# Summing the state products of a selective scan: accumulating transfers in place of GpSimd additions

## The chip, the cores and the metric

The kernel runs on one core of a Trainium2 chip. The metric is the device time in microseconds, the median of several executions. The core has TensorE (PE in the profile), VectorE (DVE), ScalarE (ACT), GpSimd (POOL) and SyncE (SP, which here only issues transfers). Each engine runs its own instructions in the order in which they were recorded, and waits for others through semaphores. DMA engines move data beside them; a transfer is issued by an instruction on the queue of some engine and tells its landing by a semaphore.

## The reference

The input x is 4 sequences of 1024 tokens with 128 channels. Four blocks are added to it one after the other, each behind a layer norm: sparse attention, a feed-forward net with weights of plus and minus one, a Mamba block, and the same feed-forward net again. The change is in the scan of the Mamba block:

```
def step(h, inp):
    dt_t, B_t, C_t, u_t = inp
    dA = jnp.exp(dt_t[..., None] * A)
    h = dA * h + (dt_t * u_t)[..., None] * B_t[:, None, :]
    y_t = jnp.einsum('ben,bn->be', h, C_t)
    return (h, y_t)
...
y = ys.transpose(1, 0, 2) + u2 * D_param
y = y * jax.nn.silu(z)
out = jnp.einsum('ble,ed->bld', y, W_out)
return x + res_scale * out
```

There are E = 256 inner channels and N = 16 states. For each token and inner channel, y is the sum over the 16 states of state times C, plus the skip term u2 * D. All of it is float32.

## The kernel before

**Stages.** First comes the attention, up to about 245 us. After the weights of the other blocks are loaded, the first feed-forward pieces and the first Mamba inputs are made, and then the scan stage runs. All the rest of the work, most of the two feed-forward blocks and the Mamba projections among it, is put between the scans in small pieces. Behind the scans comes the last feed-forward batch, which needs the last scan's output.

**Units.** Inner channels lie on the 128 partitions in NH = 2 halves, and 512 tokens (CH) lie along the free axis. One unit is one state n of one half sequence (b, f): 4 sequences x 2 halves x 16 states = 128 units, in the order of `parts_in_order`, the state innermost. `scans` (from line 1134) records the units one after the other. In unit i:

- `load_b` (line 1142) issues on SP, every second unit, the transfer of two states' B rows to all partitions (`bs`, 512 KB).
- `drive(i + 2)` makes on GpSimd `db` = dt * u * B for two units ahead. There are three `db` buffers, so this product waits for the scans of unit i - 1.
- TensorE spreads the row of C over all partitions (`pcc`, one PSUM bank, so that it waits for the product of unit i - 1).
- VectorE runs two scans, one for each half: `hs` from `da` (PSUM, made by ScalarE in `decay`) and `db`.
- VectorE multiplies both halves at once: `hc` = `hs` * `pcc`, a tile of 128 x 1024 float32, 512 KB:

```
hss[i] = m2.tile([P, NH, CH], F32, name=f"hc{i}", tag="hc", bufs=6)
ve.tensor_tensor(hss[i], hs, pc.unsqueeze(1).to_broadcast([P, NH, CH]), ALU.mult)
```

**The sum over states.** Products are added in pairs. For an even unit k, `fold` adds `hc` of unit k into `hc` of unit k + 1 on GpSimd, one half at a time (128 x 512), in units k + 2 and k + 3. `total` then adds the pair's sum into a PSUM bank `pys` with a matmul by the identity, one half at a time, in units k + 3 and k + 4; the first addition of a half sequence is preceded by a matmul with `skip_d`, the skip term. After the 16th state `gated` multiplies `pys` into the gate tile on VectorE, in units k + 4 and k + 5 for the last pair. The gate then goes to the output projection (`mamba_out`, `mamba_out_own`).

**What sets the order.** The kernel's engines are wrapped so that instructions stay in the order recorded. Between a unit's scans and its product, and behind the product, `pieces` places side work. It keeps a modelled clock for each engine, which `spend` advances by the expected duration of what was recorded, and rates of side work that each engine is owed per unit (`RATES`, line 1278). So whatever changes the modelled clocks or the moment at which a gate is finished also changes where later pieces stand.

**Buffers.** The six `hc` buffers are handed out again in the order in which they are released, a buffer being released by the last recorded reader of its tile. PSUM has three banks for side work (`SPARE`), two for `da`, one for `pcc`, and one for each half's `pys`.

Of the kernel before, what the change touches and what calls it, by code (L numbers as in the profile page):

```python
# [16 lines left out]
F32 = mybir.dt.float32  # L17
# [5 lines left out]
ALU = mybir.AluOpType  # L23
# [3 lines left out]
P = 128  # L27
# [10 lines left out]
E, N, DC, DR = 256, 16, 4, 8  # L38
NH = E // P
CH = 512  # L40
# [3 lines left out]
def hybrid_kernel(ctx: ExitStack, tc: tile.TileContext, x, Wq, Wk, Wv, Wo, ln_g, ln_b, W_in, conv_w,  # L44
# [17 lines left out]
    ve, te, sc, gp = (InOrder(e) for e in (nc.vector, nc.tensor, nc.scalar, nc.gpsimd))  # L62
# [32 lines left out]
    ident = const.tile([P, P], F32, name="ident")  # L95
# [611 lines left out]
    with tc.tile_pool(name="kload", bufs=1) as kl:  # L707
# [7 lines left out]
        total = fw.tile([P, 1], F32, name="total")  # L715
# [16 lines left out]
    fed = set()  # L732
# [166 lines left out]
    skip_d = mw.tile([P, NH, P], F32, name="skip_d")  # L899
# [13 lines left out]
    units = [(b, f, n) for b, f in parts_in_order for n in range(N)]  # L913
    PER = N
    mamba_in, mamba_pre, prepared = {}, {}, set()
# [218 lines left out]
    def scans(wide, ready):  # L1134

        bss, dbs, das, hss = {}, {}, {}, {}
        py = {}
        last = len(units) - 1  # L1140

        def load_b(i):

            if i <= last and i % 2 == 0:
                b, f, n = units[i]
                ready(b, f, "b")
                bss[i] = m2.tile([P, 2, CH], F32, name=f"bs{i}", tag="bs", bufs=2)
                nc.sync.dma_start(bss[i], mamba_pre[b, f][5][n : n + 2, :].partition_broadcast(P))

        def drive(i):  # L1150
            if i <= last:
                b, f, n = units[i]
                ready(b, f, NH - 1)
                dbs[i] = m2.tile([P, NH, CH], F32, name=f"db{i}", tag="db", bufs=3)
                bs = bss[i - n % 2][:, n % 2]
                gp.tensor_tensor(dbs[i], mamba_pre[b, f][3], bs.unsqueeze(1).to_broadcast([P, NH, CH]), ALU.mult)

        def decay(i, h):
            if i <= last:
                b, f, n = units[i]  # L1160
                das[i, h] = wide.tile([P, CH], F32, name=f"da{i}_{h}", tag="da", bufs=2)
                sc.activation(das[i, h], mamba_pre[b, f][2][:, h], AF.Exp, scale=a_t[:, h, n : n + 1])

        def fold(i):

            h = i % 2
            k = i - 2 - h
            if 0 <= k <= last:
                gp.tensor_add(hss[k + 1][:, h], hss[k + 1][:, h], hss[k][:, h])

        def total(i):

            h = 1 - i % 2
            k = i - 3 - h
            if not 0 <= k <= last:
                return
            b, f, n = units[k]
            if n == 0:
                py[b, f, h] = wide.tile([P, CH], F32, name=f"pys{b}_{f}{h}", tag=f"pys{h}")
                te.matmul(py[b, f, h], skip_d[:, h], mamba_pre[b, f][1][:, h], start=True, stop=False)  # L1180
            te.matmul(py[b, f, h], ident, hss[k + 1][:, h], start=False, stop=n == N - 2)

        def gated(i):

            h = i % 2
            k = i - 4 - h
            if not 0 <= k <= last:
                return False
            b, f, n = units[k]
            if n == N - 2:  # L1190
                gate = mamba_pre[b, f][0]
                ve.tensor_mul(gate[:, h], gate[:, h], py.pop((b, f, h)))
                if h == NH - 1:
                    fed.add(("g", b, f))
            return n == N - 2


        done = {}

        def after(*keys):  # L1200
            return [done.get(k, 0.0) for k in keys]

        for i in range(3):
            load_b(i)
        for i in range(2):
            drive(i)
            done["db", i] = spend("gp", 2.38)
        for h in range(NH):
            decay(0, h)
            done["da", 0, h] = spend("sc", 0.7)  # L1210
        for i, (b, f, n) in enumerate(units):
            now[0] = i
            load_b(i + 3)
            fold(i)
            h0, h1 = i % 2, 1 - i % 2
            done["fold", i] = spend("gp", 1.29, *after(("hc", i - 1 - h0)))
            drive(i + 2)
            done["db", i + 2] = spend("gp", 2.38, *after(("hs", i - 1, 1)))
            pc = wide.tile([P, CH], F32, name=f"pcc{i}", tag="pcc")
            te.matmul(pc, spread[: 6 * N, n, :], mamba_pre[b, f][4], start=True, stop=True)  # L1220
            done["pcc", i] = spend("pe", 0.4, *after(("hc", i - 1)))
            hs = m2.tile([P, NH, CH], F32, name=f"hs{i}", tag="hs")
            db = dbs.pop(i)
            for h in range(NH):
                first = carry[b % 2][:, h, n : n + 1] if f else 0.0
                ve.tensor_tensor_scan(hs[:, h], das.pop((i, h)), db[:, h], first, ALU.mult, ALU.add)
                done["hs", i, h] = spend("ve", 1.235 if f else 1.175, *after(("da", i, h), ("db", i)))
            decay(i + 1, 0)
            done["da", i + 1, 0] = spend("sc", 0.67, *after(("hs", i, 0)))

            t = times["ve"]
            pieces(t + 2.5, lumps=False)
            if f == 0:
                sc.copy(carry[b % 2][:, :, n : n + 1], hs[:, :, CH - 1 :])
            decay(i + 1, 1)
            done["da", i + 1, 1] = spend("sc", 0.67 if f else 0.86, *after(("hs", i, 1)))
            if gated(i):
                spend("ve", 0.68, *after(("sum", i - 1)))
            hss[i] = m2.tile([P, NH, CH], F32, name=f"hc{i}", tag="hc", bufs=6)
            ve.tensor_tensor(hss[i], hs, pc.unsqueeze(1).to_broadcast([P, NH, CH]), ALU.mult)  # L1240
            done["hc", i] = spend("ve", 1.205, *after(("pcc", i)))
            total(i)
            done["sum", i] = spend("pe", 1.0, *after(("fold", i - 1)))
            t = times["ve"]
            pieces(t + 2.2)
        for i in range(last + 1, last + 6):
            fold(i)
            gated(i)
            total(i)


    SPARE = 3
# [3 lines left out]
    def spend(engine, us, *others):  # L1256
        times[engine] = max(times[engine], *others, 0.0) + us
        return times[engine]
# [36 lines left out]
    def pieces(until, lumps=True):  # L1295

        forced = not until
        evictions(lumps, forced)  # L1300
        for k, rate in RATES.items():
            owed[k] = min(max(owed[k], -2 * rate) + (0 if forced else rate / 2), rate / 2)
        left = SPARE - sum(w.held for w in works)

        for w in works[:-2] + sorted(works[-2:], key=lambda w: w.count):

            moved = w in emptied and now[0] < len(units) - 10
            while w.may() and not w.next.evict and w.next.banks <= left:
                if moved and not w.next.same and not (forced and w in emptied):
                    break  # L1310
                if not (forced or w.next.hurries()):
                    if any(us and owed[k] <= 0 for k, us in w.next.us.items()):
                        break
                    if "pe" in w.next.us and ends(w)[0]["pe"] > until:
                        break
                left -= w.next.banks
                issue(w)
                moved = True
            if forced and moved:
                break  # L1320

    def ready(*part):
        while part not in prepared:
            pieces(None)

    def stream(*kinds):
        for k in kinds:
            yield from k
# [23 lines left out]
    with banks(8):  # L1352
        first = [
            Work(stream(*(mamba_norm(0, c) for c in first_half))),
            Work(mamba_pre_half(*parts_in_order[0])),
        ]
# [18 lines left out]
    with banks(SPARE), tc.tile_pool(name="wide", bufs=1, space=PSUM) as wide:  # L1375
# [21 lines left out]
        ])  # L1397
        among_scans[0] = True
        scans(wide, ready)
        among_scans[0] = False  # L1400
        works.insert(0, Work(mamba_out_own(B - 1, 1)))
# [40 lines left out]
```

## Time and profile before

| | |
|---|---|
| runs | 905.14, 903.53, 904.64 us; median 904.64 |
| profiled execution, from the first to the last instruction | 901.9 us; of its own time outside the span nothing is recorded, and the median of the runs is 2.7 us above the span |
| busy: PE, DVE, ACT, POOL | 756.2, 754.3, 607.1, 727.0 us (84%, 84%, 67%, 81%) |
| `db` on POOL | 128 instructions, 2.363 us each |
| additions of pairs on POOL | 128 instructions, 1.272 us each |
| products `hc` on DVE | 128 instructions, 1.218 us each |
| scans on DVE | 256 instructions, 1.207 us (first half sequence) and 1.266 us (second) each |
| transfers of the 16 DMA engines | 53.18 MB; 20.4% of their time on the queue of SP, 0.2% on that of POOL |

In the rows, an instruction is named by engine, operation and tiles (out<-in). Nearly every one has line 57, since one helper records them all, so it is read by tiles. A float32 matmul of 512 columns is two records of PE. Instructions that issue a transfer are not counted as busy time of their engine. Times are from the span's start.

### The profile page before, as it was taken

Reading aid. Unit: us, or ns where it says so; the run is one execution under the profiler, and the core shown is the slowest. Engines: PE = TensorE matmul, PEld = TensorE weight load, DVE = VectorE, ACT = ScalarE, POOL = GpSimd, SP = SyncE. Lnnn points to the kernel's source line nnn. Section 1 sums busy time; section 2 is a strip of 40 time slices with the busy share of each in tenths; the row PEclk is TensorE's granted clock in tenths of the full one; section 3 lists DMA queues with packets and bytes.
Section 4 is the critical chain, followed back from the end, with each engine's and each line's share of the span. In section 5 each row is a group of like instructions: output and inputs, shape, how many; then the busy total and the mean of one; then the engine's idle time right before and its main releaser. Section 6 shows DMA issues by size and latency. Waiting matters only on the chain. (4 is left out here: it accounts for less than half of the span.)

```text
span 901.9 us, 16464 instructions
## 1 busy us (share of the span) xinstructions
PE 756.2 (84%) x6226; PEld 463.5 (51%) x6226; DVE 754.3 (84%) x994; ACT 607.1 (67%) x1358; POOL 727.0 (81%) x566
## 2 busy tenths in 40 slices
PE   5897779866798978879899888779889989989777
PEld 2454546544577642335456554335455545656457
DVE  6799999999533289798899999989988898999962
ACT  4776648744445488888787888888777766654423
POOL 6799958998322199999999999999988987997930
PEclk9899989987789997789999999899989999999899
DMA  4733123330100111121221211212111121221100
GB/s 127 131 73 70 43 44 69 72 65 2 43 7 1 49 53 66 67 74 48 70 69 51 70 48 70 72 47 72 70 72 59 53 78 59 70 82 58 60 7 19
DMA packets 47152, 53.18 MB, mean 59 GB/s; under 512 B 4808, under 2 KB 38384, under 8 KB 47072
## 3 DMA queue, kind: packets, MB, share of 16 engines
q1 hardware_dynamic: 45904, 51.59, 20.4%
q8 instruction: 49, 0.80, 0.4%
q0 software_dynamic: 608, 0.27, 0.2%
q10 hardware_dynamic: 560, 0.26, 0.1%
q14 instruction: 31, 0.25, 0.1%
HBM read 45.82 MB, written 4.46 MB: 56 GB/s over the span
## 5 line engine op out<-in xcount | busy, mean ns | idle before, releaser
L57 POOL TENSOR_TENSOR db<-du,bs 128x1024 f32<-128x1024 f32 x128 | 302.4, 2363 | 0.1
L57 ACT ACTIVATE da<-dt,a_t 128x512 f32<-128x512 f32 x256 | 175.5, 688 | 123.2 <-DVE hs L57 122.7
L57 POOL TENSOR_TENSOR hc<-hc,hc 128x512 f32<-128x512 f32 x128 | 162.8, 1272 | 29.1 <-DVE hc L57 28.8
L57 DVE TENSOR_TENSOR hc<-hs,pcc 128x1024 f32<-128x1024 f32 x128 | 155.9, 1218 | 23.7 <-PE pcc L57 15.4
L57 DVE TENSOR_TENSOR_SCAN hs<-da,db 128x512 f32<-128x512 f32 x128 | 149.4, 1207 | 20.7 <-ACT da L57 15.5
L57 DVE TENSOR_TENSOR_SCAN hs<-da,carry,db 128x512 f32<-128x512 f32 x128 | 156.9, 1266 | 1.2 <-ACT da L57 1.2
L57 PE MATMUL pys<-hc,ident 128*128 128x512 f32 x256 | 145.3, 651 | 6.1 <-POOL hc L57 6.0
L57 POOL TENSOR_TENSOR prodv<-vS,E 128x128 f32<-128x128 f32 (+14 forms) x30 | 69.3, 2311 | 11.5 <-ACT E L57 11.3
L57 PEld LDWEIGHTS pys<-hc,ident 128*128 128x128 f32 x256 | 49.8, 208 | 53.7 <-issue 28.1
L57 PE MATMUL pcc<-bc,spread 96*128 96x512 bf16 x128 | 51.5, 402 | 29.6 <-DVE hc L57 28.7
L57 PE MATMUL pga<-h1a,w 128*128 128x512 f32 x256 | 70.5, 425 | 2.7 <-DVE h1a L57 1.9
L57 POOL TENSOR_TENSOR prod<-kv,qs 128x128 f32<-128x128 f32 (+14 forms) x30 | 71.1, 2369 | 0.8 <-DVE or L57 0.8
L57 ACT ACT_TABLE_LOAD x48 | 61.6, 1283 | 3.5 <-issue 2.6
L57 PE MATMUL pc<-mxnT,w_conv 128*128 128x512 f32 x128 | 61.5, 606 | 2.0 <-ACT gate L57 2.0
L57 PEld LDWEIGHTS pga<-h1a,w 128*128 128x128 f32 x256 | 49.3, 195 | 25.5 <-issue 4.7
L57 ACT ACTIVATE E<-S 128x512 f32<-128x512 f32 (+15 forms) x62 | 26.5, 473 | 39.7 <-DVE S L57 39.5
L57 PE MATMUL ps<-kx,qT 64*32 64x256 f32 x1008 | 43.5, 416 | 5.8 <-DVE S L57 5.0
L57 POOL TENSOR_TENSOR du<-dt,u 128x512 f32<-128x512 f32 x16 | 20.4, 1275 | 30.5 <-ACT dt L57 30.5
L57 ACT COPY ep<-pt 128x512 f32<-128x512 f32 x32 | 18.7, 586 | 35.8 <-DVE eo L57 35.5
L57 PEld LDWEIGHTS pc<-mxnT,w_conv 128*128 128x128 f32 x128 | 24.6, 194 | 33.9 <-issue 26.7
L57 PE MATMUL pgb<-h1b,w 128*128 128x512 f32 x128 | 37.5, 439 | 4.8 <-DVE h1b L57 3.3
L57 PE MATMUL pgc<-h1c,w 128*128 128x256 f32 (+1 forms) x192 | 37.2, 346 | 0.0
(244 smaller groups left out, 1637.5 us busy)
## 6 DMA issues: line engine op xcount, KB each, us to landing
bs<-bd SPq DMA_DIRECT2D x64, 512.0 KB
vr<-vd SPq DMA_DIRECT2D x32, 256.0 KB
vd<-kv SPq DMA_DIRECT2D x8, 256.0 KB
x<-in_L_attn_a_x_dram SPq DMA_DIRECT2D x15, 128.0 KB
kx<-kT SPq DMA_DIRECT2D x104, 16.0 KB
out_dram<-x SPq DMA_DIRECT2D x8, 128.0 KB
taps<-in_L_attn_b_conv_w_dram SPq DMA_DIRECT2D x1, 512.0 KB
out_dram<-ox SPq DMA_DIRECT2D x2, 256.0 KB
```

The source lines that it names most:

```text
L57: ins = getattr(self.engine, name)(*args, **kwargs)
```

## The change

For units k to k + 3 with k divisible by four, three accumulating transfers issued on GpSimd's queue add the products, both halves at once (128 x 1024, 512 KB each): product k into k + 1 (issued in unit k + 2), k + 2 into k + 3 (unit k + 4), and then k + 1 into k + 3 (unit k + 6, which waits for the other two). They are recorded in `gather`, behind `drive`. `total` adds product k + 3, now the sum of four, into `pys`, half 0 in unit k + 7 and half 1 in unit k + 8. The gate multiplications of a half sequence come in units k + 8 and k + 9 of its last four, two units later than before. The last four units of all are exempt (`alone`): TensorE adds each of their products by itself, and the gates follow at once. The modelled durations change with it: 0.9 us of GpSimd for each transfer instead of 1.29 us for each addition, and 1.0 us of TensorE for each addition that is recorded instead of 1.0 us in every unit.

```diff
-        def fold(i):
-
-            h = i % 2
-            k = i - 2 - h
-            if 0 <= k <= last:
-                gp.tensor_add(hss[k + 1][:, h], hss[k + 1][:, h], hss[k][:, h])
-
-        def total(i):
-
-            h = 1 - i % 2
-            k = i - 3 - h
-            if not 0 <= k <= last:
-                return
+        def alone(k):
+            return k > last - 4
+
+        def gather(i):
+
+            count = 0
+            for k, to, quarter in ((i - 6, 2, (0,)), (i - 2, 1, (0, 2))):
+                if 0 <= k <= last and units[k][2] % 4 in quarter and not alone(k):
+                    src = k + 1 if to == 2 else k
+                    gp.dma_start(hss[src + to], hss[src], accum_op=ALU.add)
+                    count += 1
+            return count
+
+        def add(k, h):
+
             b, f, n = units[k]
-            if n == 0:
+            first = (b, f, h) not in py
+            if first:
                 py[b, f, h] = wide.tile([P, CH], F32, name=f"pys{b}_{f}{h}", tag=f"pys{h}")
                 te.matmul(py[b, f, h], skip_d[:, h], mamba_pre[b, f][1][:, h], start=True, stop=False)
-            te.matmul(py[b, f, h], ident, hss[k + 1][:, h], start=False, stop=n == N - 2)
+            te.matmul(py[b, f, h], ident, hss[k][:, h], start=False, stop=n == N - 1)
+            return 2.0 if first else 1.0
+
+        def total(i):
+
+            us = 0.0
+            for h in range(NH):
+                k = i - 4 - h
+                if 0 <= k <= last and units[k][2] % 4 == 3 and not alone(k):
+                    us += add(k, h)
+            if alone(i - 1):
+                us += sum(add(i - 1, h) for h in range(NH))
+            return us
 
         def gated(i):
 
-            h = i % 2
-            k = i - 4 - h
-            if not 0 <= k <= last:
-                return False
+            for h in range(NH):
+                k = i - 5 - h
+                if 0 <= k <= last and units[k][2] == N - 1 and not alone(k):
+                    gate_by(k, h)
+                    return True
+            return False
+
+        def gate_by(k, h):
             b, f, n = units[k]
-            if n == N - 2:
-                gate = mamba_pre[b, f][0]
-                ve.tensor_mul(gate[:, h], gate[:, h], py.pop((b, f, h)))
-                if h == NH - 1:
-                    fed.add(("g", b, f))
-            return n == N - 2
+            gate = mamba_pre[b, f][0]
+            ve.tensor_mul(gate[:, h], gate[:, h], py.pop((b, f, h)))
+            if h == NH - 1:
+                fed.add(("g", b, f))
...
-            fold(i)
-            h0, h1 = i % 2, 1 - i % 2
-            done["fold", i] = spend("gp", 1.29, *after(("hc", i - 1 - h0)))
             drive(i + 2)
             done["db", i + 2] = spend("gp", 2.38, *after(("hs", i - 1, 1)))
+            for _ in range(gather(i)):
+                spend("gp", 0.9, *after(("hc", i - 1)))
...
-            total(i)
-            done["sum", i] = spend("pe", 1.0, *after(("fold", i - 1)))
+            done["sum", i] = spend("pe", total(i))
             t = times["ve"]
             pieces(t + 2.2)
-        for i in range(last + 1, last + 6):
-            fold(i)
-            gated(i)
-            total(i)
+        total(last + 1)
+        for h in range(NH):
+            gate_by(last, h)
```

## The prediction

> **What bounds the kernel now.** I first cut the trace into windows at the first scan, at the end of the last product with C, and at the start of the last feed-forward batch. Columns: stretch, its length, then busy time of PE, weight loads, DVE, ACT and POOL with instruction counts, granted clock, DMA share, GB/s.
>
> ```profile
> 318.75:866.45 547.70, 472.12 (x1710) 265.10 (x1708) 504.58 (x493) 409.34 (x869) 508.76 (x378) 0.92 0.19 63
> 866.45:884.05 17.60, 14.88 (x104) 11.70 (x104) 5.10 (x17) 3.98 (x11) 3.74 (x4) 1.00 0.03 8
> ```
>
> Everything that changes lies in the first of these stretches, the scan stage: 128 units of one state each, 547.7 us, 4.28 us a unit. POOL (93%) and DVE (92%) look equally loaded, so the shares cannot say which one sets the pace. The timeline of DVE in a quiet stretch does:
>
> ```profile
> 802.42 1.22 DVE L57 TENSOR_TENSOR hc<-hs,pcc 128x1024 f32<-128x1024 f32 x1
> 803.56 2.45 DVE L57 TENSOR_TENSOR_SCAN hs<-da,carry,db 128x512 f32<-128x512 f32 x2
> 806.11 1.22 DVE L57 TENSOR_TENSOR hc<-hs,pcc 128x1024 f32<-128x1024 f32 x1
> 807.25 2.45 DVE L57 TENSOR_TENSOR_SCAN hs<-da,carry,db 128x512 f32<-128x512 f32 x2
> ```
>
> The reader is to see the starts: scan 803.56, scan 807.25, so a unit with no side work takes 3.69 us, with no gap on DVE. Scan, product, scan is the chain; every DVE piece put between lengthens it. What DVE waits for in the stage is then the whole of what this change can win there. The waits view of DVE in that window (us in total, times, longest):
>
> ```profile
> DVE hs L57 <- ACT da L57: 16.7, 15, 8.3
> DVE hc L57 <- PE pcc L57: 15.4, 16, 2.9
> DVE x L57 <- PE pfob L57: 3.2, 3, 2.0
> DVE hs L57 <- POOL db L57: 3.0, 3, 1.6
> DVE hs L57 <- POOL hc L57: 2.1, 1, 2.1
> ```
>
> The 8.3 is the wait before the first scan, outside the stage. Inside: 8.4 on ACT, 20.8 on PE (15.4 + 3.2 + 0.8 + 0.7 + 0.7, the last three from rows not shown), 5.1 on POOL. With some 9 us of hand-overs of 0.1 us that is the stage less DVE's busy time, 547.7 - 504.6 = 43.1. POOL, although 93% busy, delays DVE by 5.1 us only: its products `db` are mostly 2 to 7 us early.
>
> **The change, part by part.** *POOL loses the folds.* From the groups of instructions:
>
> ```profile
> L57 POOL TENSOR_TENSOR hc<-hc,hc 128x512 f32<-128x512 f32 x128 | 162.8, 1272 | 29.1 <-DVE hc L57 28.8
> L57 PE MATMUL pys<-hc,ident 128*128 128x512 f32 x256 | 145.3, 651 | 6.1 <-POOL hc L57 6.0
> ```
>
> 128 folds, 162.8 us, go. Three transfers for each group of four states, with the last group left out (31 groups), put 93 issues on the same queue. The nearest rows are the issues on POOL before the stage: 0.54 us (`kx`, eight rows), 0.70 to 0.75 (128 rows in two runs), 1.15 (the first, after a pause). I take 0.75, nearest in shape: 70 us, bounds 50 to 107. POOL falls from 508.8 to about 416 us of the stage and stays ahead; of its 5.1 us of waits I take 4 away (bounds 0 and 5.1; two short ones may come back where a statistics block stands before a `db`).
>
> *TensorE adds half as often.* 128 additions `pys<-hc` (two records each) become 31 x 2 for the groups and 4 x 2 for the last four units, 70. Records of one matmul start 0.43 us apart, so 0.87 us each: 58 fewer are 50 us of queue; by busy time (145.3/128 = 1.14) 66. What that is worth is not the sum but where PE's queue is longer than DVE's unit, because `pcc`, the broadcast of C, stands in that queue. I laid both programs' PE orders beside their DVE orders, summed matmul times between one `pcc` and the next by such spacings, and took off the DVE work of the same unit. The queue of the stage falls from 455 to 401 us. Before, 46 intervals are longer than their unit, by 46 us in all; after, 39, by 23. Halved excess, halved waits: 10.4 of the 20.8 us (bounds 0 and 20.8). DVE's and ACT's instructions are the same in number, so ACT's 8.4 us stays.
>
> *Each transfer moves 512 KB and becomes a new wait.* No accumulating transfer is in the trace. The nearest row is the plain 512 KB load of B:
>
> ```profile
> 601.65:604.05 2.40, 0.85 (x2) 0.02 (x1) 2.40 (x3) 2.22 (x6) 2.23 (x5) 1.00 0.69 218
> ```
>
> The SyncE issue at 600.69 was followed by 218 GB/s for 2.40 us. Small POOL transfers landed 2.0 to 3.6 us after their issue began (`w_xp`), about 1.5 after it ended. So from the issue's start: 0.75 + 1.5 + 2.4 = 4.7 us if accumulating costs nothing more, and 7.1 if it takes the data time twice. Slower cannot be excluded by any row: the longest landing of a POOL transfer seen is 7.4 (`kx`, the last of eight queued). I take 5.9, the middle, since the destination is read as well as written.
>
> The Trainium skill (Collectives: The Full Stack, the bandwidth ceiling: the fold count and why AG ≠ RS ≠ AR) speaks against the change here: an add in the DMA path is limited by its two source reads and moves half of what a copy moves. By it the landing would be near the 7.1 us, and the time that of rival B; no run here shows an accumulating transfer yet.
>
> What is late if it is late: the six `hc` buffers are handed out in the order of release, so with two transfers to be landed a unit's product `hc` overwrites a buffer that a transfer issued two units earlier still read. The issue can begin when `db` of that unit is through, 2.36 us after a scan's end; from there to the product two units on (the third product after that scan) the trace of before has 9.4 us at least, 11.1 on average. PE must also add (0.87) and run `pcc` (0.39) and perhaps a piece of 1.2 us between the landing and that product. So up to about 8.6 us nothing on DVE waits. Behind the waiting issue on POOL stand `db` and the next issue, covered by the lead of `db`. On PE the addition for half 0 waits for the last transfer, and the feed-forward pieces and the next `pcc` are queued behind it: the transfer lands 2.4 + 5.9 = 8.3 us after that scan, PE gets there after one unit, a product and some 2 us of pieces, 4.28 + 1.2 + 2 = 7.5. So PE is held 0.8 us, 25 us over 31 groups, of the 147 us that PE then has free (547.7 - 401). I put 2 us of it on the path (bounds 0 and 10.4).
>
> *The end.* The gates come two units later, so feed-forward pieces slip behind the scans. Behind the last `pcc` stand 33.0 us of matmuls before and 36.6 after: two groups of eight `pgc` more, and additions of the last units. Against that goes the wait for the last folds:
>
> ```profile
> 867.84 2.35 PE L57 MATMUL pys<-hc,ident 128*128 128x512 f32 x4 [1.52 <-POOL hc L57]
> ```
>
> PE is 14.88 of 17.6 us busy there, so more work is longer time. Between -1.5 (only the wait goes) and +3.7; I take +3, since the work is in the order that I read.
>
> **The sum.** -4 (POOL) - 10.4 (PE) + 2 (PE held) + 3 (end) = -9.4 us. On the profiled span, 901.9, that is 892.5; the median of the runs is 904.64, 2.7 us over the span, which is taken as unchanged: 895 us.
>
> **The rivals.** *A, late transfers, slower.* If an accumulating transfer lands later than 8.6 us after its issue, the product two units on waits, once a group at least. At 10 us the wait is 1.4 us in 31 groups, 43 us: 938. For it: no row bounds the accumulation from above, and three transfers of 512 KB join 64 loads of the same size. Against: the DMA share is 0.19 in the stage, and the load went at 218 GB/s. *B, gain eaten.* At about 7.1 us PE is held 2 us a group, 62 us; PE's queue is back at 401 + 62 = 463 us, over the 455 of before, and DVE's waits on PE return: -4 + 3, 901 on the span, 904. For it: the upper of the two sums from the load's row. Against: the 2 us of pieces ahead of PE's addition are a mean, and PE had 75 us of idle time in the stage before. *C, larger gain.* Transfers land by 5 us and nearly all waits on PE and POOL go: -25.9 + 3, 879 on the span, 882. Against: 23 us of excess remain in the order.
>
> **How the numbers follow.** Forecast 0.55, A 0.25, B 0.12, C 0.08. From no change a measurement tells 0.2%, 1.8 us. The forecast gives 0.52 faster and 0.03 same, C 0.08 faster, B 0.02, 0.05 and 0.05, A 0.25 slower: faster 0.62, same 0.08, slower 0.30. The forecast's own range is 882 to 902 (all of the 20.8 us on PE at one end, none at the other). For 8 in 10 I go down to C's 882 and up into A to 922, a landing of about 9.4 us; beyond is the slower part of A, some 0.15, and little below.
>
> **What would show it.** Right: `pys` at 140 records, POOL's folds gone and DMA issues of 0.5 to 1.2 us in their place; landings of 4.7 to 7.1 us; DVE's wait for `pcc` near 8 us and for `db` near 1; the scan stage near 535 us and the stretch to the last batch near 20.6. Wrong: `hc` on DVE waiting for a DMA; additions on PE whose longest wait is for the transfer; issues over 1.2 us, with `db` late; or a scan stage no shorter although POOL is idle.

## The result and the profile after

The changed kernel is slower: 916.58 us (median of 6 runs, 911.89 to 918.36) against 906.61 us for the kernel before (6 runs, 903.53 to 909.69), a ratio of 1.0097 with a 95% interval of 1.0067 to 1.0126. The forecast, 895 us, had the wrong sign. The profiled execution took 918.36 us, with a span of 916.6 us.

The same two stretches as before, in windows of the profile after (length, then busy time of PE, weight loads, DVE, ACT and POOL with instruction counts, granted clock, DMA share, GB/s):

```profile
322.80:874.90 552.10, 444.15 (x1572) 251.68 (x1571) 504.10 (x493) 406.96 (x865) 437.52 (x345) 0.85 0.67 151
874.90:898.80 23.90, 20.34 (x128) 16.99 (x126) 5.19 (x17) 5.84 (x15) 1.26 (x2) 0.86 0.02 6
```

The scan stage is 4.4 us longer (552.1 against 547.7), the stretch to the last batch 6.3 us (23.9 against 17.6); together 10.7 us, close to the 10.0 us between the medians. DVE's busy time is unchanged (504.1 against 504.6), so the stage grew by idle time of DVE, 43.1 to 48.0 us. POOL's busy time fell by 71 us: 162.8 us of folds are gone, and the 93 issues stand in their place, since issues on GpSimd's queue are counted as busy time in these rows (85.9 us in the row below), unlike what is said of issues above. And the granted clock of TensorE fell from 0.92 to 0.85: although 58 additions are gone, PE's busy time fell by 28 us only.

What lies before the stage has the same instructions in all kernels here and took 318.2 to 323.7 us from one profile to another. So I compare stages, not spans, in single profiles, and leave verdicts to the medians.

The groups and the transfer issues of the page (busy time, mean ns of one, idle time just before; for the issue row KB of each and median us to landing):

```profile
L57 POOL TENSOR_TENSOR db<-du,bs 128x1024 f32<-128x1024 f32 x128 | 315.9, 2485 | 58.1 <-DVE hs L57 31.4
...
L57 PE MATMUL pys<-hc,ident 128*128 128x512 f32 x140 | 85.0, 702 | 14.8 <-DMA hc<-hc 14.8
L57 POOL DMA_DIRECT2D hc<-hc x93 | 85.9, 1002 | 7.1 <-DVE hc L57 3.4
...
hc<-hc POOLq DMA_DIRECT2D x93, 512.0 KB, 4.8
```

The 93 issues and the 140 records are as predicted. An issue takes 1.0 us, and the median landing is 4.8 us, faster than the 5.9 of the sum. One record of an addition grew from 651 to 702 ns: the same instruction, at a lower clock.

The waits in the stage (us in total, times, longest):

```profile
PEld pys L57 <- DMA hc<-hc: 29.8, 11, 5.4
...
DVE hc L57 <- PE pcc L57: 24.2, 15, 3.4
DVE hs L57 <- ACT da L57: 17.8, 12, 8.3
...
PE pys L57 <- DMA hc<-hc: 14.8, 10, 2.8
...
DVE hs L57 <- POOL rs_fb L57: 1.0, 1, 1.0
```

DVE's waits on POOL fell from 5.1 to 1.0 us. Its wait for `pcc`, forecast near 8 us, rose from 15.4 to 24.2. No product waits for a transfer, so rival A's mechanism is absent. The additions do wait for transfers, in 10 places, as the prediction's list of bad signs has it. One of them in the timeline:

```profile
598.96 2.34 DVE L57 TENSOR_TENSOR_SCAN hs<-da,db 128x512 f32<-128x512 f32 x2 [0.41 <-ACT da L57]
...
604.73 1.84 POOL L57 DMA_DIRECT2D hc<-hc  x2
...
606.24 0.59 PE L57 MATMUL pcc<-bc,spread 96*128 96x512 bf16 x1 [0.62 <-DVE hc L57]
...
609.64 2.08 PE L57 MATMUL pys<-hc,ident 128*128 128x512 f32 x2 [2.82 <-DMA hc<-hc]
...
611.65 3.77 PE L57 MATMUL pd<-dtl,w_dt 8*128 8x512 f32 x4
...
615.36 0.61 PE L57 MATMUL pcc<-bc,spread 96*128 96x512 bf16 x1
...
616.00 1.22 DVE L57 TENSOR_TENSOR hc<-hs,pcc 128x1024 f32<-128x1024 f32 x1 [3.41 <-PE pcc L57]
```

PE stands 2.82 us at the addition, until the transfer issued at 604.73 has landed. Behind it on PE's queue is a piece (`pd`), and behind that the next `pcc`. And all of it runs at half speed: the addition takes 2.08 us where two such records take 1.02 at full clock, `pcc` 0.61 instead of 0.38. DVE, free from 612.6, gets its `pcc` 3.41 us late. The hold and the half rate are not to be told apart here: the hold is 2.82 us, and at full clock the addition, `pd` and `pcc` would have taken about 3.2 us less (an estimate, half of their time). Of the 15 waits for `pcc` only two, 6.3 of 24.2 us, have a held addition between that `pcc` and the one ahead of it. Windows of 3.41 us around that place show the clock:

```profile
599.89:603.31 3.42, 1.75 (x6) 0.35 (x5) 3.33 (x4) 3.04 (x6) 3.34 (x4) 1.00 0.45 86
603.31:606.72 3.41, 1.11 (x3) 0.18 (x2) 3.31 (x4) 2.94 (x8) 3.41 (x4) 0.50 0.87 201
606.72:610.13 3.41, 0.59 (x2) 0.49 (x2) 3.32 (x4) 3.38 (x9) 3.41 (x2) 0.50 1.02 195
610.13:613.55 3.42, 3.42 (x5) 0.87 (x5) 2.46 (x3) 2.88 (x11) 3.04 (x4) 0.50 1.04 236
...
627.20:630.61 3.41, 3.41 (x14) 1.80 (x13) 3.07 (x5) 2.38 (x8) 2.59 (x3) 1.00 0.88 232
```

The second column is PE's busy time, the one with 1.00 and 0.50 the granted clock. In 599.89 to 603.31 PE is busy for 1.75 of 3.42 us; the clock is then halved, stays at half through the hold, and through the burst of work that had gathered behind it, until 627.2. Added up over the stage, TensorE ran at half rate for 85.3 us before and for 163.8 us after.

### The profile page after: what moved, and what is told of

Read it like the earlier page. It is cut to its first block, busy times and chain, and to the rows that moved or that the text cites. A ratio compares the mean times of both kernels' runs of the same rounds, so it can differ in the third digit from the quotient of the medians.

```text
span 916.6 us, 16264 instructions
## 1 busy us (share of the span) xinstructions
PE 733.9 (80%) x6110; PEld 455.8 (50%) x6110; DVE 754.0 (82%) x994; ACT 606.7 (66%) x1358; POOL 653.4 (71%) x531
## 3 DMA queue, kind: packets, MB, share of 16 engines
q0 software_dynamic: 14000, 49.03, 29.4%
q1 hardware_dynamic: 45904, 51.59, 19.6%
## 5 line engine op out<-in xcount | busy, mean ns | idle before, releaser
L57 POOL TENSOR_TENSOR db<-du,bs 128x1024 f32<-128x1024 f32 x128 | 315.9, 2485 | 58.1 <-DVE hs L57 31.4
L57 DVE TENSOR_TENSOR hc<-hs,pcc 128x1024 f32<-128x1024 f32 x128 | 156.0, 1219 | 31.6 <-PE pcc L57 24.2
L57 PE MATMUL pys<-hc,ident 128*128 128x512 f32 x140 | 85.0, 702 | 14.8 <-DMA hc<-hc 14.8
L57 POOL DMA_DIRECT2D hc<-hc x93 | 85.9, 1002 | 7.1 <-DVE hc L57 3.4
L57 PE MATMUL pcc<-bc,spread 96*128 96x512 bf16 x128 | 54.6, 427 | 44.3 <-DVE hc L57 43.4
L57 PE MATMUL pga<-h1a,w 128*128 128x512 f32 x256 | 74.6, 447 | 0.2
L57 PE MATMUL pc<-mxnT,w_conv 128*128 128x512 f32 x128 | 64.4, 640 | 6.8 <-DVE h1a L57 2.7
L57 PEld LDWEIGHTS pga<-h1a,w 128*128 128x128 f32 x256 | 53.3, 211 | 25.2 <-issue 4.0
L57 PEld LDWEIGHTS pys<-hc,ident 128*128 128x128 f32 x140 | 29.1, 223 | 52.3 <-DMA hc<-hc 29.8
L57 POOL TENSOR_TENSOR du<-dt,u 128x512 f32<-128x512 f32 x16 | 24.5, 1534 | 31.6 <-ACT dt L57 31.6
```

Source lines behind the costliest of these rows:

```text
L57: ins = getattr(self.engine, name)(*args, **kwargs)
```

## Theories

*Clock (W).* Fewer additions leave TensorE idle in more stretches; the clock is halved after them, and what comes next takes longer (in the place above an addition 2.08 us instead of 1.02, `pcc` 0.61 instead of 0.38). The queue, counted at full clock, is shorter, but not in time. *Hold (H).* PE stands at an addition until the last transfer lands, with `pcc` behind it. *Order (O).* Gates told two units later push pieces behind the last scan. The rival to W is the prediction's own *queue (Q)*: half the additions, half the waits, with the transfers spoiling it.

## Experiments

All comparisons are with the kernel before, on the same chip, 5 rounds each. Stage lengths and half-rate time come from one profile each.

**Half the additions, no transfers** (kernel before):

```diff
-            te.matmul(py[b, f, h], ident, hss[k + 1][:, h], start=False, stop=n == N - 2)
+            if n % 4:
+                te.matmul(py[b, f, h], ident, hss[k + 1][:, h], start=False, stop=n == N - 2)
```

> The kernel before, in which TensorE leaves out half of its additions (the pairs that begin with a state divisible by four are not added, so their part of the sum is missing); the order on every engine is else that of before. Theory W (the clock): with less work TensorE has more idle windows, so the half-rate time in the scan stage rises from 85 us to 130 us or more, busy time of PE falls by less than 45 us instead of 56 to 73, and DVE's wait for pcc stays at 12 us or more: time between -5 and +5 us of before. Theory Q (the queue, as predicted): a shorter queue halves DVE's waits on PE, and the time falls by about 10 us.

906.84 us, ratio 1.0007 (0.9990 to 1.0024): no gain. The window of the stage, whose length is that of before:

```profile
322.30:869.80 547.50, 434.63 (x1582) 251.52 (x1580) 504.96 (x493) 409.39 (x869) 508.67 (x378) 0.88 0.18 63
```

Half-rate time rose from 85.3 to 133.1 us, and DVE's wait for `pcc` fell from 15.4 to 12.8 only. DVE's waits on PE in all fell by 2.7 us (20.8 to 18.1), and those on ACT rose by 1.5 (8.4 to 9.9). So the term of -10.4 us would not have come even with no transfer in the kernel.

**The changed kernel without its transfers:**

```diff
-                    gp.dma_start(hss[src + to], hss[src], accum_op=ALU.add)
```

> The kernel after without its 93 transfers (only every fourth product enters the sum); the orders of PE, DVE and ACT are those of after. Theory W: the half-rate time stays near 164 us, and DVE's wait for pcc stays at 18 us or more; only what PE was held by transfers goes, 3 to 6 us faster than after. Theory H (the hold): DVE's wait for pcc falls from 24 to 14 us or less and the time by 10 us or more, to that of before or under it. Theory O (the order of the side work): no change over 3 us, and the stretch to the last batch stays near 24 us.

905.64 us, ratio 0.9998 (0.9978 to 1.0018). The changed kernel stood 10 us above the kernel before; the 93 transfers carry all of it, in net. In its profile the stage is 544.8 us instead of 552.1 while the stretch to the last batch is still 24.0: the end is not the transfers' doing. Its waits in the stage:

```profile
DVE hc L57 <- PE pcc L57: 14.2, 13, 2.7
DVE x L57 <- PE pfob L57: 3.6, 2, 3.1
DVE x L57 <- PE pfoa L57: 2.5, 3, 1.6
```

The wait for `pcc` is 14.2 us, with 150.2 us at half rate. H had forecast 14 us or less, W 18 or more and 3 to 6 us of time: W's figures missed. So the rise from 15.4 to 24.2 came with the transfers, and the longer half-rate time alone does not give it. What W does say holds: with 58 additions fewer and no transfer, DVE's waits on PE are 20.3 us in all, against 20.8 before.

**The changed kernel with 62 more matmuls by a zero weight**, in the places of additions that it had dropped:

```diff
+            for h in range(NH):
+                k = i - 5 - h
+                if 0 <= k <= last and units[k][2] % 4 == 0 and not alone(k):
+                    extra(k, h)
...
+            te.matmul(py[b, f, h][:64], nought, w_in, start=False, stop=False)
```

> The kernel after with 62 more matmuls that add zero times a resident tile to pys, about where the additions that after dropped stood, with nothing to wait for. Theory W: the half-rate time falls from 164 us to 110 or less, DVE's wait for pcc falls under 20 us, and the time is 3 to 8 us under after although PE has 54 us more queue. Theory Q: 54 us more queue cost about 10 us, so the time is 5 to 12 us over after. Theory H: no change of more than 3 us, since the waits for transfers stay.

918.40 us, ratio 1.0139 (1.0117 to 1.0162). Half-rate time went back to 88.7 us as W says, but DVE's wait for `pcc` rose to 32.3 us: fillers keep the clock and stand in the way of `pcc`. The time is 2 to 4 us over the changed kernel (by the medians and by the ratios), where W had forecast 3 to 8 less, Q 5 to 12 more and H no change over 3. No gain, against my hope.

**First-level transfers only**, TensorE adding every second product, gates one unit later than before instead of two:

```diff
-            for k, to, quarter in ((i - 6, 2, (0,)), (i - 2, 1, (0, 2))):
+            for k, to, quarter in ((i - 2, 1, (0, 2)),):
...
-                k = i - 4 - h
-                if 0 <= k <= last and units[k][2] % 4 == 3 and not alone(k):
+                k = i - 3 - h
+                if 0 <= k <= last and units[k][2] % 2 == 1 and not alone(k):
```

> Only the first level by transfers: product k into k+1, for all pairs but the last two; TensorE adds every second product as before, half 0 in unit k+4 and half 1 in k+5, gates one unit later than before. Theory W: PE's work and its half-rate time (90 us or less) are those of before, POOL's waits are gone, and the time is 0 to 6 us under before. Theory H: the additions still wait for transfers, twice as many of them, and the time is over before by 5 us or more. Theory O: near before, within 3 us.

901.15 us, ratio 0.9956 (0.9939 to 0.9974): faster than before. Its windows:

```profile
320.11:858.77 538.66, 469.33 (x1669) 260.71 (x1668) 502.18 (x487) 406.66 (x857) 410.12 (x314) 0.92 0.50 124
858.77:881.84 23.07, 21.31 (x154) 17.59 (x153) 7.40 (x24) 8.03 (x23) 1.26 (x2) 1.00 0.05 16
```

The clock is back at 0.92, and no addition waits for a transfer. The stage is 9 us shorter than before, the end 5.5 us longer: PE has 154 instructions there, not 104, at full clock.

**The changed kernel with additions one unit later** (21 of 31 groups; the planner's numbers as they were):

```diff
-                k = i - 4 - h
-                if 0 <= k <= last and units[k][2] % 4 == 3 and not alone(k):
-                    us += add(k, h)
+                for k, inner in ((i - 5 - h, True), (i - 4 - h, False)):
+                    if 0 <= k <= last and units[k][2] % 4 == 3 and not alone(k):
+                        if inner == (units[k][2] != N - 1 and k <= last - 16):
+                            add(k, h)
```

> The changed kernel, but the addition of a group of four into pys is recorded one unit later in 21 of the 31 groups (all but the last group of a half sequence, so that gates and the order of all other work stay). If the hold is real (TensorE stands at the addition until the third transfer has landed, and the next pcc is queued behind it), the waits of PE and its weight loads on hc<-hc, 14.8 and 29.8 us, fall to about a third, and the scan stage goes from 552.1 to about 547 us (with no transfers at all it was 544.8): some 912 us. If the 7 us come from the transfers themselves in another way (db slower beside them, the clock), the stage stays at 551 to 553 us and the time at 916.

909.95 us, ratio 1.0047 (1.0029 to 1.0065), 6 us less than the changed kernel. Waits in its stage:

```profile
DVE hc L57 <- PE pcc L57: 21.1, 17, 3.2
...
PEld pys L57 <- DMA hc<-hc: 10.2, 4, 3.8
PE pys L57 <- DMA hc<-hc: 8.2, 3, 2.8
```

The weight loads' wait fell to a third, PE's to 8.2 in three places (a third had been expected), the stage to 547.4 us. H holds, and is worth some 4.5 us by the ratios, 6 by the medians, with three of the ten waits still there.

**The gate told two units later** (kernel before, gate multiplications unmoved):

```diff
-                    fed.add(("g", b, f))
+                    told.append((i + 2 if k < last - 1 else i, ("g", b, f)))
```

> The kernel before, but the planner is told two units later that a half sequence's gate is finished (the gate multiplications stay where they were; the last half sequence is told at once). If the order of the pieces makes the end longer, the stretch from the last product to the last batch goes from 17.6 to 23 or 24 us with a scan stage near 547: about 912 us. If the longer end of the changed kernel comes from the single additions of its last four units, the stretch stays at 17.6 us and the time at 905.

912.25 us, ratio 1.0066 (1.0043 to 1.0089). The stage is 547.4 us; the stretch behind it:

```profile
868.01:892.20 24.19, 20.66 (x133) 17.33 (x132) 5.19 (x18) 6.12 (x16) 3.75 (x4) 0.90 0.02 6
```

This is the end of the changed kernel, with nothing else of it in place. O holds: 6.1 us by the medians.

**First-level transfers, with the last two products of a half sequence added one by one**, so that gates stand as before:

```diff
-                k = i - 3 - h
-                if 0 <= k <= last and units[k][2] % 2 == 1 and not alone(k):
-                    us += add(k, h)
+                for k, ns in ((i - 3 - h, range(1, N - 2, 2)), (i - 1 - h, (N - 2,)), (i - 2 - h, (N - 1,))):
+                    if 0 <= k <= last and units[k][2] in ns and not alone(k):
+                        us += add(k, h)
```

> The kernel with the first level of transfers alone (TensorE adds every second product), but the last two products of a half sequence are added by TensorE one by one, so that its gates stand in the units in which they stood in the kernel before. If the end depends on when a gate is told, the stretch to the last batch falls from 23.1 to between 17.6 and 20 us and the scan stage stays near 539: 896 to 898 us, faster than both. If the short scan stage of that kernel was bought with the work that slipped behind it, the stage grows by what the end loses, and the time stays at 901.

910.59 us, ratio 1.0049 (1.0028 to 1.0069), missed by both theories. The end came down to 20.0 us, but the stage went from 538.7 to 550.5, with 22.4 us of waits for `pcc` and 4.5 for a piece on ACT. A few additions and numbers of the planner changed move a stage by 11.8 us, as much as anything tried here, so the 538.7 may have been partly luck of its order; no run separates that.

**Half the additions, and fillers where TensorE stood idle** (53 of the 59 that the plan lists; the other six fall where no sum is open, and `if opened else 0` leaves them out):

```diff
+            for _ in range(IDLE.get(i - 1, 0) if opened else 0):
+                te.matmul(opened[-1][:64], nought, w_in, start=False, stop=False)
             pc = wide.tile([P, CH], F32, name=f"pcc{i}", tag="pcc")
```

> The kernel before without half of its additions (as in the run that left them out), and with 59 matmuls by a zero weight, put only into units in which that run's TensorE stood idle just ahead of pcc, up to three in a unit; all other engines' orders are unchanged. Part of the sum is left out. If the clock took the gain (half rate after 3.4 us stretches in which TensorE is idle), half-rate time in the scan stage falls from 133 to 90 us or less, DVE's wait for pcc from 12.8 to about 8, and the stage from 547.5 to about 542: 901 us. If a shorter queue is simply worth nothing here, or the fillers themselves come in the way of pcc, the stage stays at 547 to 550: 906 us or more.

913.33 us, ratio 1.0075 (1.0052 to 1.0098). Half-rate time fell to 78.5 us, under that of before; the wait for `pcc` rose to 22.4 and the stage to 555.7. W's positive form, a short queue at full clock, could not be made this way.

**16 of 128 additions left** (kernel before):

```diff
-            te.matmul(py[b, f, h], ident, hss[k + 1][:, h], start=False, stop=n == N - 2)
+            if n == N - 2:
+                te.matmul(py[b, f, h], ident, hss[k + 1][:, h], start=False, stop=True)
```

> The kernel before with only 16 of its 128 additions into pys (the last one of each half sequence and half), so that most of the sum is left out; the skip matmuls stay, and all other engines' orders are unchanged. If the length of TensorE's queue decides, and the run with half of the additions only missed it by chance, DVE's wait for pcc falls well under 12.8 us, to some 5, and the scan stage from 547.5 to about 540: 899 us. If the clock takes it back, half-rate time in the stage rises over 133 us, to 160 or more, the wait for pcc stays above 10, and the stage stays at 545 to 549: 905 us.

909.09 us, ratio 1.0036 (1.0012 to 1.0059): with 112 additions fewer, and nothing put in their place, the kernel is slower.

```profile
323.72:875.24 551.52, 411.29 (x1486) 246.09 (x1484) 504.89 (x493) 409.58 (x869) 508.67 (x378) 0.82 0.18 63
```

DVE, ACT and POOL have the counts of before; the clock fell to 0.82, half-rate time rose to 199.5 us. With 128, 64 and 16 additions the half-rate time is 85, 133 and 200 us and the stage 547.7, 547.5 and 551.5. Over whole executions the granted clock was 0.911 to 0.930 in all 23 of the kernel before, 0.886 to 0.899 in the 12 with half of the additions, and 0.848 to 0.867 in the 12 with 16. Q cannot give that. But the wait for `pcc` is not where the time went: it is 11.6 us here, and DVE's waits on PE in all are 20.5 (20.8 before). The 3.8 us by which the stage grew are waits on ACT (8.4 to 10.4 us), on POOL (5.1 to 6.2) and small gaps, in a profile of an execution of 914.24 us, the longest of this kernel's; the 545 to 549 us that W had forecast were missed.

**First-level transfers in the order of before:**

```diff
-            if 0 <= k <= last:
+            if 0 <= k < last - 1:
+                if h == 0:
+                    gp.dma_start(hss[k + 1], hss[k], accum_op=ALU.add)
+            elif 0 <= k <= last:
                 gp.tensor_add(hss[k + 1][:, h], hss[k + 1][:, h], hss[k][:, h])
```

> The kernel before with each pair added by one accumulating transfer, issued where the first half of the pair was added on GpSimd; the last pair of all stays on GpSimd, and PE's, DVE's and ACT's orders and the planner's numbers are those of before, additions one by one as before. If the 9 us shorter scan stage of the kernel with the first level alone came from GpSimd's waits (5.1 us here) and shorter queue on GpSimd, this one keeps it with the end of before: stage 540 to 543, end 17.6, 897 to 900 us. If it came from the order of the pieces, only GpSimd's waits go: 543 to 545, some 902 us. If additions in unit k + 3 wait for the landing and hold pcc, the stage is 548 or more: 906 us or more.

898.76 us (895.92 to 903.00), ratio 0.9928 (0.9903 to 0.9954): the fastest version.

```profile
318.16:861.80 543.64, 469.09 (x1710) 261.21 (x1708) 504.45 (x493) 409.34 (x869) 414.00 (x315) 0.93 0.51 125
861.80:879.40 17.60, 14.90 (x104) 11.67 (x104) 5.10 (x18) 3.99 (x11) 3.74 (x4) 1.00 0.03 9
```

POOL drops by 95 us, its waits on DVE's path go (the stage is 4.1 us shorter in this profile; where the rest of the 7.2 us between the medians lies is not shown), PE keeps all additions and its clock, and the end is untouched. The 63 transfers hold five additions for 5.6 us in all, beside which the wait for `pcc` is 14.2 us.

**The changed kernel's sums in the order of before** (its transfers for the first twelve states, additions one unit later, last four states on GpSimd, gates as before):

```diff
+                if 0 <= k <= last and units[k][2] % 4 in quarter and units[k][2] < 12:
+                    src = k + 1 if to == 2 else k
+                    gp.dma_start(hss[src + to], hss[src], accum_op=ALU.add)
...
+                k = i - 5 - h
+                if 0 <= k <= last and units[k][2] in (3, 7, 11):
+                    add(k, h)
```

> The changed kernel's three transfers for the first three groups of four in each half sequence, with their additions one unit later; the last four products of a half sequence are added in pairs on GpSimd as before, gates stand where they stood before, and the planner is given the numbers of before, so that DVE's and ACT's orders are those of before. If hold and order are what made the changed kernel slower than before, this one loses both: stage 544 to 547 us, end 17.6 us, 902 to 905 us in all. If the transfers or the clock cost more by themselves, the stage stays over 550 and the time over 908.

904.70 us, ratio 0.9980 (0.9958 to 1.0002). Its windows:

```profile
318.75:865.42 546.67, 443.57 (x1605) 260.62 (x1603) 504.00 (x493) 408.57 (x867) 455.38 (x354) 0.87 0.55 132
865.42:885.40 19.98, 18.75 (x116) 13.95 (x114) 5.10 (x18) 4.74 (x13) 3.76 (x4) 0.94 0.03 8
```

No addition waits for a transfer, the gates stand as before, and the changed kernel's idea is no slower than before. But the end is 20.0 us and not the 17.6 expected: additions of the last group of transfers now stand behind the last product (10 records of `pys`, 4 before), and 2.2 us run at half rate. And the kernel stands 6 us over the version above, 3.0 in the stage and 2.4 at the end. That version has the same orders on DVE and ACT; between them lie the second level and 48 additions fewer on TensorE, and half-rate time is 141 against 75 us. Which of these costs the 3.0 us of the stage is open.

## Why the prediction was wrong, step by step

- **GpSimd, -4.** Right: DVE's waits on POOL went from 5.1 to 1.0 us. The issues took 1.0 us instead of 0.75, within the bounds, and nothing came of that.
- **TensorE's queue, -10.4.** This is the step that failed. It forecast that DVE's waits on PE fall from 20.8 to 10.4 us when half of the additions go. In the three kernels with fewer additions and no transfers they were 18.1 us (64 additions fewer), 20.3 (58 fewer, in the changed kernel's order) and 20.5 (112 fewer), with 133, 150 and 200 us at half rate instead of 85; the stage of the first was 547.5 us, that of before 547.7. So the term is measured as about nothing. The reason is in part argued. "Halved excess, halved waits" took all matmul times at one clock, from spacings of 0.43 us. In the trace of before, 9 of the 16 waits for `pcc` have half-rate work between that `pcc` and the one ahead of it; had that work run at full clock, up to about 9 of the 15.4 us would be gone. That would leave some 6.5 us of them for a shorter queue to halve. And the half-rate part is not fixed: after the change 13 of 15 waits have it, up to about 19 of 24.2 us. This points at the clock and not at the count of the queue. What a half queue at a held clock would give was not measured, since both attempts to hold the clock lengthened the queue.
- **PE held by the transfer, +2.** Wrong in price: some 4.5 to 6 us. PE waited less in all than assumed (14.8 us, not 25), and the landings were shorter (4.8 us, not 5.9), by which the prediction's own sum has no hold at all: 2.4 + 4.8 is under 7.5. In the place shown the issue began 3.4 us after the scan's end (601.30), not 2.4, and PE was at the addition 5.5 us after it (606.82), not 7.5: no piece stood ahead. I also set the hold against PE's 147 us of free time, and it does not fall there: it falls ahead of the pieces and the `pcc` that have gathered behind it, and while it lasts PE is idle, which in the windows shown kept the clock at half. Additions one unit later returned 6 us by the medians, no transfers at all 10 (905.64 against 916.58, in different comparisons with before). Rival B had named this hold, and priced it at 904 by landings of 7.1 us; landings were 4.8.
- **The end, +3.** Right in sign and in the work that it counted, half the size: 6.3 us, and 6.1 from telling the gate later alone. The sum counted 3.6 us more matmuls behind the last `pcc`, at full clock. In the stretch PE is busy 20.3 instead of 14.9 us, and 6.8 us of it have the half clock. PE is busy in 5.8 of these, so about 2.9 us of the 5.5 are the clock and 2.6 more work. Here too the clock was the part left out.
- **The sum.** By the medians: order +6.1, hold +6.2, and what is left of the 10.0 measured, -2.3, which holds the -4 of GpSimd. By the ratios it is 6.0, 4.5 and -1.7 of 8.8. The range "882 to 902" was reckoned on the span of 901.9 us; on the median, as the forecast is, the same two bounds give 885 to 906.
- **Rival A** failed on its condition: the longest landing is 8.0 us, under the 8.6 that it needed, and no product waited. **Rival C** failed although its condition, landings by 5 us, was met by the median: the queue's waits did not go.

The Trainium skill (Collectives: The Full Stack, the bandwidth ceiling) says of reduce-scatter in a ring that the add in the DMA path is limited by its two source reads. The prediction carried this over to a transfer within SBUF. The 4.8 us here is close to the 4.7 that a plain transfer's rate gave, so in landing time the rule does not show. In the engines' time something of it may: after the change the 49.03 MB on the queue of the accumulating transfers took 29.4% of the DMA engines' time, the 51.59 MB on SP's queue 19.6%.

## What to carry to other kernels

Count the queue of TensorE at the clock that it will have: where it shares its time with idle stretches, matmuls taken out can lower the clock for all that is left. Here 58 to 112 additions fewer took between 0.3 and 2.7 us off DVE's waits on PE, and bought nothing. A sum moved into transfers pays where it frees an engine that others wait for and touches no order: one level in place of GpSimd's additions was worth 0.7%; with the second level, and the fewer additions that come with it, that gain was gone. A consumer recorded one step too early for its transfer stalls what is queued behind it, and a planner told later of a finished piece moves work behind the end: try both alone before judging the main idea.

## What the runs showed of the hardware

- **The clock.** In all records here the granted clock is 1.0 or 0.5, in steps of 3.413 us. I cut the scan stages of the 13 profiles into such windows and took PE's busy share in each at full clock, and the clock of the next. Under 0.4 busy, 123 of 123 were followed by half rate; from 0.4 to 0.5, 57 of 73; from 0.5 to 0.6, 33 of 86; from 0.6 to 0.8, 16 of 253; above, 12 of 1088. From half rate, full clock came back only after windows at least 0.8 busy (241 of 323; 0 of 128 below). The Trainium skill (TensorE: Matmul & The Clock Gate, Part 1: The HAM clock gate) gives the same two rates and window, and asks for an idle window before the clock is halved; here windows suffice in which TensorE is half idle, such as the one of 599.89 above.
- **Accumulating transfers within SBUF.** In the changed kernel 55 of the 64 that did not follow another at once landed 4.5 to 5.0 us after the issue began, the other nine up to 8.0; the 29 that were second of two issued back to back took 6.5 to 8.0 us. No plain transfer within SBUF is in the traces to set beside them.
- **GpSimd beside them.** `db` grew from 2.363 to 2.485 us on average beside the 93 transfers, and to 2.615 in the fastest version, where a transfer is issued just ahead of it. Scans and products on DVE kept their times (1.22 us a product in each).
